# A two-layer kernel with m's norm by rows, group statistics in steps, six C products a chunk on GpSimd, and deferred transposes in layer 1

## The chip, the cores and the metric

The kernel runs on one core of a Trainium2 chip. The time is the device time of one execution in microseconds (us). PE is TensorE's matmul, PEld its weight load, DVE is VectorE, ACT ScalarE, POOL GpSimd, SP SyncE, whose queue issues most DMAs.

## The reference

`x` is 2 x 512 x 64 x 64 in float32, seen as 2 images of 4096 tokens with 512 channels. All arithmetic is float32.

```python
# layer 0: x = x + mamba(_gn(x)), _gn: group norm, 32 groups of 16 channels
xn = (xf - mu) * rsqrt(var + EPS) * ln_w + ln_b          # norm over the 512 channels of a token
xin, z = split(xn @ in_proj_w.T)                          # 1024 and 1024
xc = silu(causal_conv(xin, conv_w, 4 taps) + conv_b)
x_dbl = xc @ x_proj_w.T                                   # dt (32), B (16), C (16)
delta = softplus(dt @ dt_proj_w.T + dt_proj_b)
h = exp(delta * A) * h + delta * xc * B                   # scan over 4096 tokens, 1024 x 16 states
y = sum_n(h * C) + xc * D_skip
x = x + (y * silu(z)) @ out_proj_w.T
# layer 1: x = x + memory(_gn(x)), m: 1024 x 512
score = l2norm(xf) @ l2norm(m).T
idx = argmax(score)                                       # one row of m per token
emean = segment_sum(xf, idx) / (counts + 1e-6)
new_m = m * 0.999 + emean * 0.001
x = x + softmax(score) @ new_m
```

## The kernel before

Layer 0 goes through 32 chunks (2 images, 16 chunks of T = 256 tokens). A chunk is 32 units: 8 blocks of 128 inner channels by 4 groups of 4 states. A unit is a tile 128 x 4 x 256. For unit k:

- `decay`: ACT makes dA = exp(delta*A), four activations, into PSUM (dA, two buffers);
- `feed`: POOL multiplies bu = B * du (128 x 4 x 255) into one of LEAD = 4 buffers, four units ahead; `first` sets the first column on ACT;
- `scan`: DVE scans dA and bu, in place in PSUM, then `weigh` makes hc = dA * C on DVE;
- `gather`: PE sums hc over the states by eight transposes into yT.

Units whose number in the chunk is in `AT["aside"]` are different: the scan writes into the SBUF tile dS (tile h, pool s1, one buffer), and POOL makes the product hc one unit later. There are two buffers hc. `carry` copies of the last state are on ACT. Around the units stand the projections of the next chunk (front: pz, xi, the convolution cv, px, the softplus in `soft` with q on POOL and DVE, z), the norm of the chunk after it (`norms`), and the output product of the chunk before (`back`: po, xo, written to x1d). All of these are cut into small functions with a place: the dictionary AT gives the unit at which each is issued, a table sorted by unit and priority is worked off in the loop at L962, and the layer's engines run in exactly this order (class InOrder). That's why nearly all of layer 0 has line L36 in the profile.

Besides, at given chunks: `stats_end(1)` in chunk 0 and `end` in the chunk after an image's last one compute group statistics (`group_stats`: aggregates, two small matmuls with gmat, a reciprocal root) in one go; `unit_m` in chunks 8 to 11 normalizes a quarter of m, columns of a transposed copy mT, with a matmul by meanc for the squared lengths, and writes mnd; `clear` zeroes the two tables tab; `prelude` in the last chunk loads and normalizes the first tile of layer 1 (xf0, on POOL).

Layer 1 has two stages, in 16 tiles of TT = 512 tokens. Matching (L1108): for each of the 64 subtiles of 128 tokens 8 float32 matmuls give pc (scores, 128 x 1024); ACT copies it to sc and makes ex = exp; DVE scales ex by the reciprocal of den and takes max and max_index. One subtile later `match` makes a 128 x 128 matrix sel of equal indices (dg on ACT, pr on PE, sel on DVE) and `add_rows` gathers rows of a table, adds pe = sel x xT and counts, and scatters them back; two tables alternate. `exT_part` transposes ex of the subtile before in two halves (px, one PSUM buffer, then a copy on ACT), and a full tile exT is written to exd in DRAM. The output stage (L1173): `new_m` for 8 blocks of m from both tables (tiles e), then po = new_m x exT per tile, with exT read back from exd in two buffers (pool q3), added to xt and stored. In the first pair of tiles the blocks of new_m are interleaved with the matmuls.

Of the kernel before, what the change touches and what calls it, by code (L numbers as in the profile page):

```python
# [18 lines left out]
P = 128  # L19
# [30 lines left out]
def kernel(  # L50
# [15 lines left out]
    mT: bass.AP,  # L66
# [76 lines left out]
    def rsqrt(nc, dst, var, work):  # L143

        nc.scalar.activation(dst, var, AF.Ln, bias=epsc)
        nc.scalar.activation(dst, dst, AF.Exp, scale=-0.5)
        nc.vector.tensor_mul(work, dst, dst)
        nc.vector.scalar_tensor_tensor(work, var, EPS, work, ALU.add, ALU.mult)
        nc.vector.tensor_scalar(work, work, -0.5, 1.5, ALU.mult, ALU.add)
        nc.vector.tensor_mul(dst, dst, work)  # L150

    def group_stats(nc, st, mu, rs, pool, psum):

        mv = pool.tile([P, CB, 2], F32, tag="gs_mv", name="gs_mv")
        for cb in range(CB):
            nc.vector.bn_aggr(mv[:, cb, :], st[:, cb].rearrange("p n s -> p (n s)"))
        w = pool.tile([P, CB, 2], F32, tag="gs_w", name="gs_w")
        pm = psum.tile([P, 2, T], F32, tag="mm", name="gs_pm")
        nc.vector.tensor_copy(w[:, :, 0], mv[:, :, 0])
        nc.tensor.matmul(pm[:, 0, :CB], gmat, w[:, :, 0], start=True, stop=True)  # L160
        nc.vector.tensor_copy(mu, pm[:, 0, :CB])
        d = pool.tile([P, CB], F32, tag="gs_d", name="gs_d")
        nc.vector.tensor_sub(d, mv[:, :, 0], mu)
        nc.vector.tensor_mul(d, d, d)
        nc.vector.tensor_add(d, d, mv[:, :, 1])
        pv = psum.tile([P, 2, T], F32, tag="mm", name="gs_pv")
        nc.tensor.matmul(pv[:, 0, :CB], gmat, d, start=True, stop=True)
        d2 = pool.tile([P, CB], F32, tag="gs_d2", name="gs_d2")
        rsqrt(nc, rs, pv[:, 0, :CB], d2)
# [4 lines left out]
    with ExitStack() as l0:  # L174
# [5 lines left out]
            "u": (-10, -8, -2, 1), "xi": (-9, -4, 0, 2), "c": (-6, -3, 2, 5), "o": (-4, -2, 4, 6),  # L180
            "x": 10, "xo": 13, "z": (17, 18, 19, 21), "zo": (19, 20, 22, 26),
            "soft": (20, 21, 22, 23, 23, 25, 26, 27), "silu": 9, "early": -105,
            "aside": (2, 8, 12, 16, 26), "gate": 3,
            "norm": (-4, 3, 3, 8, 10, 11, 14, 15, 15, 16, 20, 20),
            "back": ((2, 6, 8, 11), (2, 12, 14, 18)), "end": 23, "u1": (3, 4, 7, 9),
            "xi1": (5, 6, 8, 10), "c1": (7, 9, 10, 12), "o1": (8, 10, 11, 13), "x1": 15,
            "xo1": 17, "silu1": 13, "gate1": 6, "z1": (1, 2, 3, 6),
            "soft1": ((-5, -3, -3, 1, 2, 3, 3), (3, 3, 5, 5, 5, 7, 8), (7, 7, 9, 9, 15, 17, 19)),
            "wo": (5, 1, 8, 7), "m": (2, 28, 28, 30, 31, 32), "gs": 14, "zo1": (2, 3, 4, 7),
            "norm1": (0, 0, 0, 0, 0, 1, 1, 2, 2), "affine": 0,  # L190
# [24 lines left out]
        def stats_end(b):  # L215
            group_stats(nc, st0, gmu[0][b], grs[0][b], s1, ps)
            nc.vector.tensor_mul(gsh[b], gmu[0][b], grs[0][b])
            nc.vector.tensor_scalar_mul(gsh[b], gsh[b], -1.0)
# [180 lines left out]
        stats_end(0)  # L399
# [210 lines left out]
        def back_fns(i):  # L610
# [38 lines left out]
            def end():  # L649
                if c == NCH - 1:  # L650
                    group_stats(nc, sts[b], gmu[1][b], grs[1][b], s1, ps)
                state[i].clear()
# [3 lines left out]
        def back(i):  # L656
# [10 lines left out]
            return parts + [(AT["end"], end)]  # L667

        def unit_m(q):

            s = {}
            cols = slice(q * T, (q + 1) * T)

            def load_m():
                s["m"] = s1.tile([P, CB, T], F32, tag="m", name="m")
                nc.sync.dma_start(
                    s["m"], mT[:, cols].rearrange("(cb p) k -> p cb k", p=P)
                )

            def square(h):  # L680
                sq = s1.tile([P, 2, T], F32, tag="sq", name="sqm")
                nc.scalar.activation(sq, s["m"][:, 2 * h : 2 * h + 2], AF.Square)
                if h == 0:
                    s["pn"] = ps.tile([P, 2, T], F32, tag="mm", name="pn")
                for j in range(2):
                    cb = 2 * h + j
                    nc.tensor.matmul(
                        s["pn"][:, 0], meanc, sq[:, j], start=cb == 0, stop=cb == CB - 1
                    )

            def root():
                s["r"] = s1.tile([P, 2, T], F32, tag="sq", name="rm")
                r, ss = s["r"][:, 0], s["r"][:, 1]
                nc.vector.tensor_scalar(
                    ss, s.pop("pn")[:, 0], float(C), 1e-24, ALU.mult, ALU.max
                )
                nc.scalar.activation(r, ss, AF.Ln)
                nc.scalar.activation(r, r, AF.Exp, scale=-0.5)

            def newton():  # L700
                r, ss = s["r"][:, 0], s["r"][:, 1]
                nc.gpsimd.tensor_mul(ss, ss, r)
                nc.gpsimd.tensor_mul(ss, ss, r)
                nc.gpsimd.tensor_scalar(ss, ss, -0.5, 1.5, ALU.mult, ALU.add)
                nc.gpsimd.tensor_mul(r, r, ss)

            def scale():
                m = s["m"]
                nc.gpsimd.tensor_mul(m, m, s.pop("r")[:, 0:1].to_broadcast([P, CB, T]))
                nc.sync.dma_start(mnd[:, :, cols], m)  # L710

            return list(zip(AT["m"], (
                load_m, lambda: square(0), lambda: square(1), root, newton, scale
            )))

        def clear():

            zrow = s1.tile([P, CB, T], F32, tag="m", name="zrow")
            nc.gpsimd.memset(zrow, 0.0)
            for tab in tabs:  # L720
                for kb in range(KB):
                    nc.sync.dma_start(
                        tab[kb * P : (kb + 1) * P],
                        zrow.rearrange("p n t -> p (n t)")[:, :ROW],
# [198 lines left out]
        M_AT = [len(chunks) // 4 + q for q in range(K // T)]  # L923
# [13 lines left out]
        for i in range(len(chunks)):  # L937
# [14 lines left out]
            if i > 0:  # L952
                table += [(at + n, 4, fn) for n, fn in back(i - 1)]
# [4 lines left out]
        table.append((AT["gs"], 5, lambda: stats_end(1)))  # L958
# [35 lines left out]
        end()  # L994
# [4 lines left out]
    l1 = ctx.enter_context(tc.tile_pool(name="l1", bufs=1))  # L999
    ones = l1.tile([P, P], F32, name="ones")  # L1000
    nc.gpsimd.memset(ones, 1.0)
    p3 = ctx.enter_context(tc.tile_pool(name="q3", bufs=2))
    KH = K // TT
# [13 lines left out]
    with ExitStack() as s:  # L1017
        p1 = s.enter_context(tc.tile_pool(name="p1", bufs=1))
        p2 = s.enter_context(tc.tile_pool(name="p2", bufs=2))
        ps_t = s.enter_context(tc.tile_pool(name="ps_t", bufs=1, space=PSUM))  # L1020
# [50 lines left out]
        def match(s, xT, i, fx, ix):  # L1071

            dg = p2.tile([P, P], F32, tag="dg", name="dg")
            nc.scalar.mul(dg, ident, fx)
            pr = ps_e.tile([P, TT], F32, tag="pe", name="pr")
            nc.tensor.matmul(pr[:, :P], ones, dg, start=True, stop=True)  # L1076
# [21 lines left out]
        late = None  # L1098

        def transpose_late(kh):  # L1100
            if late is not None:
# [47 lines left out]
        for kh in range(KH):  # L1149
            transpose_late(kh)  # L1150
# [100 lines left out]
```

## Time and profile before

| | us |
|---|---|
| median of three runs | 5042.65 (5036.36 to 5051.64) |
| the profiled execution | 5043.67, span 5042.0 |
| start, before the first scan | 108.9 |
| chunk 0 | 145.0 |
| a steady pair of chunks (19 and 20) | 118.5 and 116.7 |
| last chunk (31) | 131.3 |
| matching | 608.1 |
| from the last pc to the first po | 23.8 |
| output stage | 455.5 |

Busy over the span: PE 90%, DVE 80%, POOL 76%, ACT 70%. A share of the whole span is a mean over stages that have different limits, so the stages are to be read by themselves. In a line of the profile stand start, duration, engine, line, operation, output and inputs; what stands in brackets is how long the engine was idle before it and what ended that.

### The profile page before, as it was taken

How to read it: one execution, taken by the hardware profiler on the slowest of the kernel's cores; microseconds unless marked ns; L12 is line 12 of the kernel's file. 1: busy time of each engine (PE TensorE's matmuls, PEld its weight loads, DVE VectorE, ACT ScalarE, POOL GpSimd, SP SyncE). 2: the span in 40 equal slices, each digit the busy share in tenths (PEclk: the TensorE clock that was granted, in tenths of full speed). 3: DMA queues.
4: the chain of work that ended last, by engine and by line, in shares of the span. 5: the costliest groups of instructions: out<-in, count | busy, mean ns of one | idle time of the engine just before them, and what ended most of it. 6: DMA issues, size and time to landing. Idle time of an engine off the chain costs nothing. (4 is left out here: it accounts for less than half of the span.)

```text
span 5042.0 us, 64859 instructions
## 1 busy us (share of the span) xinstructions
PE 4516.4 (90%) x22704; PEld 3499.2 (69%) x22704; DVE 4053.2 (80%) x3390; ACT 3535.5 (70%) x8849; POOL 3822.8 (76%) x2821
## 2 busy tenths in 40 slices
PE   7888888898888899889888898989886899998999
PEld 6777777777777777777777777777775555553444
DVE  4899999998889999999999999999998755553100
ACT  3788888888888888788888888888886455551000
POOL 4899999999999999999999999999999322220000
PEclk9999999999999999999999999999997899998999
DMA  5131112122222112122222112211112344334453
GB/s 213 36 116 66 64 68 68 65 68 72 72 72 68 66 64 64 64 64 68 77 79 80 64 64 68 70 64 64 65 61 102 116 158 148 135 131 148 140 166 117
DMA packets 174399, 447.72 MB, mean 89 GB/s; under 512 B 23256, under 2 KB 77656, under 8 KB 169848
## 3 DMA queue, kind: packets, MB, share of 16 engines
q1 hardware_dynamic: 163832, 408.97, 23.9%
q0 software_dynamic: 10240, 34.61, 2.2%
q8 instruction: 179, 2.93, 0.2%
q14 instruction: 148, 1.21, 0.1%
HBM read 351.63 MB, written 91.88 MB: 88 GB/s over the span
## 5 line engine op out<-in xcount | busy, mean ns | idle before, releaser
L36 POOL TENSOR_TENSOR bu<-B,du 128x1020 f32<-128x1020 f32 (+1 forms) x1152 | 2466.9, 2157 | 120.4 <-DVE dA L36 101.6
L36 ACT ACTIVATE dA<-delta,A 128x256 f32<-128x256 f32 x4096 | 1957.8, 478 | 149.6 <-DVE hc L36 41.1
L36 DVE TENSOR_TENSOR_SCAN dA<-dA,bu 128x1024 f32<-128x1024 f32 x864 | 1977.9, 2289 | 38.4 <-ACT dA L36 23.2
L36 PE MATMUL yT<-ident,hc 128*128 128x128 f32 x8192 | 1062.7, 278 | 201.3 <-DVE hc L36 113.0
L36 DVE TENSOR_TENSOR hc<-dA,C 128x1024 f32<-128x1024 f32 x864 | 1058.2, 1225 | 163.7 <-PE yT L36 75.1
L36 PEld LDWEIGHTS yT<-ident,hc 128*128 128x128 f32 x8192 | 950.1, 143 | 288.4 <-DVE hc L36 139.5
L36 PE MATMUL pz<-x,win 128*128 128x256 f32 x4096 | 937.4, 382 | 33.9 <-ACT bu L36 22.4
L36 PEld LDWEIGHTS pz<-x,win 128*128 128x128 f32 x4096 | 762.8, 191 | 142.5 <-POOL bu L36 25.5
L36 PE MATMUL po<-z,wo 128*128 128x256 f32 x2048 | 521.2, 413 | 0.8 <-DVE z L36 0.8
L36 PE MATMUL cv<-xi,cd 128*128 128x256 f32 x2048 | 474.4, 385 | 28.3 <-POOL xi L36 22.2
L36 PEld LDWEIGHTS po<-z,wo 128*128 128x128 f32 x2048 | 422.7, 210 | 81.3 <-issue 15.3
L1186 PE MATMUL po<-exT,win 128*128 128x512 f32 x1024 | 444.2, 597 | 20.2 <-DVE win L1169 14.7
L36 PEld LDWEIGHTS cv<-xi,cd 128*128 128x128 f32 x2048 | 382.9, 192 | 90.5 <-POOL xi L36 27.9
L1119 PE MATMUL pc<-win,xf 128*128 128x512 f32 x960 | 432.3, 592 | 0.0
L1186 PEld LDWEIGHTS po<-exT,win 128*128 128x128 f32 x1024 | 196.0, 192 | 267.8 <-issue 267.3
L1093 POOL DMA_INDIRECT tab<-rows,ix x64 | 62.7, 979 | 418.4 <-DVE den L1134 398.7
L36 POOL TENSOR_TENSOR hc<-h,C 128x1024 f32<-128x1024 f32 x160 | 379.0, 2369 | 0.2 <-PE yT L36 0.2
L36 ACT COPY carry<-dA 128x4 f32<-128x4 f32 x810 | 129.8, 160 | 347.5 <-DVE hc L36 341.7
L36 DVE TENSOR_TENSOR_SCAN h<-dA,bu 128x1024 f32<-128x1024 f32 x160 | 364.8, 2280 | 10.4 <-ACT dA L36 8.6
L1203 DVE TENSOR_TENSOR xt<-xt,po 128x512 f32<-128x512 f32 x64 | 43.9, 686 | 388.4 <-PE po L1186 373.6
L1119 PEld LDWEIGHTS pc<-win,xf 128*128 128x128 f32 x960 | 173.0, 190 | 172.2 <-issue 172.2
L36 PE MATMUL py<-ident,ys 128*128 128x128 f32 x512 | 85.2, 291 | 188.1 <-DVE q L36 79.6
(161 smaller groups left out, 5059.5 us busy)
## 6 DMA issues: line engine op xcount, KB each, us to landing
B<-bcd SPq DMA_DIRECT2D x128, 512.0 KB, 4.0
C<-bcd SPq DMA_DIRECT2D x128, 512.0 KB, 4.0
wo<-in_out_wT_dram SPq DMA_DIRECT2D x128, 512.0 KB, 4.6
exd<-exT SPq DMA_DIRECT2D x16, 2048.0 KB, 6.4
exT<-exd SPq DMA_DIRECT2D x16, 2048.0 KB, 9.3
xl<-in_x_dram SPq DMA_DIRECT2D x32, 512.0 KB, 9.9
x<-in_x_dram SPq DMA_DIRECT2D x32, 512.0 KB, 5.2
xo<-in_x_dram SPq DMA_DIRECT2D x64, 256.0 KB, 5.7
```

What stands on the lines that cost most here:

```text
L36: ins = call(*args, **kwargs)
L1093: nc.gpsimd.indirect_dma_start(tab, at, rows, None)
L1119: nc.tensor.matmul(pc[:, cols], xf[:, cb, i * P : (i + 1) * P], mn[:, cb, cols], start=cb == 0, stop=cb == CB - 1,)
L1186: nc.tensor.matmul(pos[j, cb], mrow[:, kb, cb * P : (cb + 1) * P], ld[j][0][:, kb], start=kb == 0, stop=kb == KB - 1,)
L1203: nc.vector.tensor_add(xt[:, cb], xt[:, cb], pos.pop((j, cb)))
```

## The change

Layer 0: (1) `AT["aside"]` gets a sixth unit, 10; most other places in AT move by a unit or a few. (2) `group_stats` becomes four functions issued one unit after the other (of them the mean's copy and the aggregates stay on DVE, the rest goes to the engine given: POOL in the middle of the layer, DVE for the first and the last). (3) `unit_m` works on 8 blocks of 128 rows of m (chunks 8 to 15): lengths by an accumulating square on ACT, five small operations on POOL, the scale on ACT, four transposes, a copy, and a write to mnd. The argument mT goes. Layer 1: (4) `match` makes pr by a transpose of a broadcast copy of fx. (5) The transposes of ex follow one subtile behind as before, but in the last six iterations none is done; seven subtiles' worth then stand after the loop: two before `match`, one before `add_rows`, four after it. ex has seven buffers; exd is written from ACT's queue. For the last subtile the scaling of ex comes after max_index. (6) In the output stage, exT uses two pools in turn, four buffers.

```diff
         AT = {
-            "u": (-10, -8, -2, 1), "xi": (-9, -4, 0, 2), "c": (-6, -3, 2, 5), "o": (-4, -2, 4, 6),
+            "u": (-10, -8, -1, 1), "xi": (-9, -6, 0, 4), "c": (-5, -3, 2, 5), "o": (-2, -1, 4, 6),
...
-            "aside": (2, 8, 12, 16, 26), "gate": 3,
-            "norm": (-4, 3, 3, 8, 10, 11, 14, 15, 15, 16, 20, 20),
-            "back": ((2, 6, 8, 11), (2, 12, 14, 18)), "end": 23, "u1": (3, 4, 7, 9),
+            "aside": (2, 8, 10, 12, 16, 26), "gate": 3,
+            "norm": (-2, 2, 3, 8, 10, 10, 11, 15, 15, 17, 19, 20),
+            "back": ((0, 6, 8, 11), (3, 13, 14, 17)), "end": 18, "u1": (3, 6, 8, 9),
...
-            "wo": (5, 1, 8, 7), "m": (2, 28, 28, 30, 31, 32), "gs": 14, "zo1": (2, 3, 4, 7),
+            "wo": (6, -4, 10, 7), "m": (9, 14, 17, 20, 28, 29), "gs": 11, "zo1": (3, 4, 6, 8),
...
-    def group_stats(nc, st, mu, rs, pool, psum):
+    def group_stats(nc, engine, st, mu, rs, pool, psum):
+        s = {}
+        def means():
...
+                nc.vector.bn_aggr(mv[:, cb, :], st[:, cb].rearrange("p n s -> p (n s)"))
...
+            nc.tensor.matmul(s["pm"][:, 0, :CB], gmat, w[:, :, 0], start=True, stop=True)
+        def variances():
+            nc.vector.tensor_copy(mu, s.pop("pm")[:, 0, :CB])
...
+            engine.tensor_sub(d, mv[:, :, 0], mu)
+            engine.tensor_mul(d, d, d)
+            engine.tensor_add(d, d, mv[:, :, 1])
...
+        def roots():
+            nc.scalar.copy(s["d"], s.pop("pv")[:, 0, :CB])
+            s["v"] = s["d"]
+            nc.scalar.activation(rs, s["v"], AF.Ln, bias=epsc)
+            nc.scalar.activation(rs, rs, AF.Exp, scale=-0.5)
+        def newton():
...
+        return [means, variances, roots, newton]
...
-        def unit_m(q):
+        def unit_m(kb):
...
+                s["m"] = s1.tile([P, C], F32, tag="m", name="m")
+                nc.sync.dma_start(s["m"], m[rows])
+            def square():
...
+                nc.scalar.activation(junk[:, :C], s["m"], AF.Square, accum_out=s["ss"][:, 0:1])
             def root():
...
+                nc.gpsimd.tensor_scalar(ss, ss, 1e-24, None, ALU.max)
                 nc.scalar.activation(r, ss, AF.Ln)
                 nc.scalar.activation(r, r, AF.Exp, scale=-0.5)
...
-            def scale():
-                m = s["m"]
-                nc.gpsimd.tensor_mul(m, m, s.pop("r")[:, 0:1].to_broadcast([P, CB, T]))
-                nc.sync.dma_start(mnd[:, :, cols], m)
+            def turn():
+                nc.scalar.mul(s["m"], s["m"], s["ss"][:, 1:2])
...
+                    nc.tensor.transpose(
+                        pt[:, cb * P : (cb + 1) * P], s["m"][:, cb * P : (cb + 1) * P], ident
+                    )
+            def store():
+                mt = s.pop("m")
+                nc.scalar.copy(mt, s.pop("pt").rearrange("p a t -> p (a t)"))
+                nc.sync.dma_start(mnd[:, :, rows], mt.rearrange("p (c k) -> p c k", k=P))
...
-        M_AT = [len(chunks) // 4 + q for q in range(K // T)]
+        M_AT = [len(chunks) // 4 + kb for kb in range(KB)]
...
-        table.append((AT["gs"], 5, lambda: stats_end(1)))
+        table += [(AT["gs"] + max(n - 1, 0), -1, fn) for n, fn in enumerate(stats_end(1))]
...
+    DEFER = 6
+        p_ex = s.enter_context(tc.tile_pool(name="p_ex", bufs=DEFER + 1))
...
-            nc.scalar.mul(dg, ident, fx)
+            nc.scalar.copy(dg, fx.to_broadcast([P, P]))
             pr = ps_e.tile([P, TT], F32, tag="pe", name="pr")
-            nc.tensor.matmul(pr[:, :P], ones, dg, start=True, stop=True)
+            nc.tensor.transpose(pr[:, :P], dg, ident)
...
         def transpose_late(kh):
-            if late is not None:
-                ex, exT, i, k = late
+            if late:
+                ex, exT, i, k = late[0]
                 exT_part(ex, exT, i, kh)
-                if kh == KH - 1 and i == SUB - 1:
-                    b, t = tiles[k]
-                    nc.sync.dma_start(exd[b][t], exT)
+                if kh == KH - 1:
+                    late.pop(0)
+                    if i == SUB - 1:
+                        b, t = tiles[k]
+                        nc.scalar.dma_start(exd[b][t], exT)
...
-                    transpose_late(kh)
+                    if k * SUB + i + DEFER < len(tiles) * SUB:
+                        transpose_late(kh)
...
+                if end:
+                    scale()
...
-        add_rows(*behind, match(*behind))
+        for kh in range(2 * KH):
+            transpose_late(kh % KH)
+        sel = match(*behind)
         for kh in range(KH):
             transpose_late(kh)
+        add_rows(*behind, sel)
+        while late:
+            for kh in range(KH):
+                transpose_late(kh)
...
         for k0 in range(0, len(tiles), FIRST):
+            pool = (p3, pr3)[k0 // FIRST % 2]
...
-                exT = p3.tile([P, KB, TT], F32, tag="exT", name="exT1")
+                exT = pool.tile([P, KB, TT], F32, tag="exT", name="exT1")
```

## The prediction

> **What bounds the kernel now.** I read the page's slices first, then busy time by window (cut at the first scan of a chunk), then the timelines of DVE and POOL inside one steady chunk, and for the last 1090 us the chain of waits. Slices:
>
> ```profile
> DVE  4899999998889999999999999999998755553100
> POOL 4899999999999999999999999999999322220000
> ```
>
> For three quarters of the span DVE and POOL are both full; then neither matters. The windows say how full (PE, PEld, DVE, ACT, POOL busy, then granted PE clock):
>
> ```profile
> 2411.30:2529.80 118.50, 106.38 (x608) 91.44 (x608) 112.44 (x75) 100.22 (x260) 113.26 (x83) 0.97 0.21 68
> 2529.80:2646.50 116.70, 103.38 (x609) 89.50 (x609) 112.49 (x75) 100.50 (x260) 113.53 (x83) 1.00 0.21 69
> 1195.60:1321.50 125.90, 111.49 (x618) 95.54 (x617) 113.13 (x75) 102.19 (x264) 118.21 (x88) 0.95 0.21 72
> 2045.90:2171.50 125.60, 109.19 (x623) 94.38 (x622) 118.30 (x88) 99.89 (x254) 113.80 (x78) 0.95 0.20 64
> 3954.60:4562.70 608.10, 603.95 (x2046) 313.37 (x2047) 330.48 (x786) 303.56 (x592) 136.73 (x125) 1.00 0.42 145
> 4562.70:4586.50 23.80, 5.62 (x21) 3.05 (x19) 8.42 (x20) 4.18 (x7) 3.18 (x3) 0.68 0.48 175
> 4586.50:5042.00 455.50, 444.15 (x1024) 195.94 (x1024) 58.77 (x99) 0.00 (x0) 0.00 (x0) 0.98 0.43 141
> ```
>
> Rows 1 and 2 are a steady pair of chunks, mean 117.6 us: DVE and POOL each lack about 4 us of it, so neither has room. Row 3 is a chunk with a quarter of m's norm (8.3 over the mean), row 4 the one with the group statistics of image 0 (8.0 over). Rows 5 to 7 are layer 1: matching, PE-bound; a hole of 23.8 us with PE busy 5.6; the output product, PE-bound again.
>
> Inside a chunk (POOL and DVE, units 8 to 11):
>
> ```profile
> 2916.25 2.36 POOL L36 TENSOR_TENSOR hc<-h,C 128x1024 f32<-128x1024 f32 x1
> 2922.16 2.38 POOL L36 TENSOR_TENSOR bu<-B,du 128x1020 f32<-128x1020 f32 x1
> 2926.09 2.38 POOL L36 TENSOR_TENSOR bu<-B,du 128x1020 f32<-128x1020 f32 x1 [1.54 <-DVE dA L36]
> ...
> 2917.48 2.29 DVE L36 TENSOR_TENSOR_SCAN dA<-dA,bu 128x1024 f32<-128x1024 f32 x1
> 2920.22 1.23 DVE L36 TENSOR_TENSOR hc<-dA,C 128x1024 f32<-128x1024 f32 x1 [0.44 <-PE yT L36]
> ```
>
> POOL's own wait comes after unit 10, where it has caught up with DVE. The waits of these two chunks by releaser: POOL 4.8 us on DVE; DVE 3.3 us on PE (yT), one of them 2.4.
>
> **The change part by part.** All sums stand against the profiled execution, 5043.67 us (span 5042.0 and 1.7 around it); the median of the runs is 1.0 below it.
>
> *Sixth C product on POOL (unit 10), steady chunks.* DVE loses one hc: 1.225 us and the 0.10 gap that stands before each, 1.33. POOL gains 2.37, starting 2.33 after the instruction before. In the 116.7 us chunk POOL waits 2.0 (1.54 at unit 11, 0.35, 0.11), so its work without waits is 114.8; in the 118.5 us chunk the same sum gives 114.8. With the product it needs 117.1. DVE without its larger waits needs 115.2, afterwards 113.9. So POOL becomes the bound, 0.5 below today's mean. Against that: the products of units 8, 10 and 12 share one buffer dS (pool s1, one buffer), so scan 10 must wait for POOL's product of unit 8. That ends at 2918.61 while scan 10 starts at 2917.48 today: 1.1 us. Scan 12 waits for the product of unit 10 likewise, by my placing 0.4. DVE then needs 115.4 and, with the 1.7 us of PE wait that every second chunk has more, 117.1 there. Two engines at one limit rarely meet it: I take 117.5, bounds 117.0 and 120. Over the 23 chunks with nothing else in them: -3.5 us, bounds -14 and +55. The moved slots (AT) change no duration; they decide waits, which the trace of before can't show. I put them inside these bounds, since every wait they can remove is in the 4 us of idle, and for chunk 31 and the start at 0, within 8 either way. The same chunk has POOL's xf0 norm (8.25 us) with DVE waiting 6.75 behind it, which stays.
>
> *m by rows.* Five chunks carry m: together 617.9 us, 29.7 over the mean. Gone per quarter: on POOL 3 products of 0.725, one of 0.40 and the scale of 2.36 (5.0), on DVE 0.43 in line behind PE's pn with 0.9 of waiting, 8 PE matmul passes. Now eight chunks have a block of 128 rows: POOL 5 operations on one column, between the rows of 0.19 (128x6 copy) and 0.25 (128x32): 1.0 us; ACT square, Ln, Exp, scale, copy (0.82, 0.19, 0.21, 0.6, 0.58): 2.4 of 16 us idle; 4 transposes of PE, 0.11 each; 2 DMAs on SP, whose queue has nothing behind them that is due within their issue of 0.4 to 0.5 us. New wait: ACT's Ln stands behind POOL's max. POOL runs up to 4 us late at that slot, and behind the Ln on ACT stand the decays of the next scans; I take 0.2 per block (0 to 2). -29.7 + 8 + 2 = -20, bounds -22 and -6.
>
> *Group statistics in steps.* In row 4 DVE spends 8.5 us from 2130.83 to 2139.35, 2.3 of it waiting for PE and ACT. It keeps the four aggregates (1.92), w and mu (0.3 to 2.7); eight small operations go to POOL (1.6 us). Chunks 16 and 17 are 11.6 over the mean; I leave 3.6: -8 (0 to -11). In chunk 0 POOL waits 10.0 us at unit 14 for the same thing, DVE 3.2: -5 (0 to -8). The last statistics stay on DVE, with one ACT copy more: +0.3, left out.
>
> *Layer 1, matching.* pr becomes a transpose: one pass for two. The chain has pr x2 at 0.22 in each of 64 subtiles and PE never rests: -0.11 x 64 = -7.0. dg stays one ACT operation of 0.40 (ACT has half its time free).
>
> *Deferred transposes.* The chain at the end of matching, and one burst of px with its copy:
>
> ```profile
> 4567.17 3.61 DMA rows<-tab,ix
> 4572.47 6.95 DMA tab<-rows,ix
> 4580.69 3.01 DMA e<-tab
> 4586.50 54.31 PE po L1186 x120
> 4640.82 8.79 DMA exT<-exd
> ...
> 4541.83 0.60 PE L1066 MATMUL px<-ident,ex 128*128 128x128 f32 x4
> 4542.46 0.58 ACT L1067 COPY exT<-px 128x512 f32<-128x512 f32 x1 [1.50 <-PE px L1066]
> 4567.67 1.02 PE L1066 MATMUL px<-ident,ex 128*128 128x128 f32 x4 [3.22 <-DVE fx L1141]
> ```
>
> Six iterations lose 8 transposes (0.87 us of PE): -5.2. Seven subtiles, 14 halves, then stand between the last pc (T = 4562.65) and po. The px pool has one buffer, so PE and ACT take turns: 0.60 + 0.58 + about 0.09 of handover = 1.27 each. In the changed kernel the first load of e waits for the landing of the last exd write, which now waits for all 14. Copies start at T+2.44 (sc 1.01, ex 1.13 and 0.21 go first); the last one ends 13 periods, 0.58, one dg (0.40) and pe (0.86) later: T+20.8; landing 6.4, issue 0.9: e is issued at T+28.1, today T+17.7. So +10.4 - 5.2 = +5.2: the cover is shorter than what it should hide. [...] The rows: at 4567.67 the burst took 1.02 us after 3.2 us of PE rest, and between 2450.0 and 2458.3 PE was busy 6.23 of 8.30 us and was granted 0.50 of the clock for the next 6.8. [...] By the rows, PE busy half the time loses the clock, the period is 1.69: +10.7. I take half of the bursts slow, 1.48: +8 (5 to 11). The sooner max_index of the last subtile gains nothing under this: the scatter lands at about T+16.
>
> *Four exT buffers.* PE waits 5.52 for exT before the second pair and then runs 3.4 us at half clock (1.7 lost): -7 (0 to -7.3). The third and fourth loads now go out between loads of e; a 2 MB load takes 9.3 us, and e for k-block 2 is needed 20 us after the first: covered, thinly.
>
> Sum: -3.5 - 20 - 8 - 5 - 7 + 8 - 7 = -42.5; 5043.7 - 42.5 = 5001, by the median 5000.
>
> **Rivals.** (1) *The chunk balances on POOL worse than I think*: lag at units 8 to 13 isn't given back, chunk 118.7 instead of 117.5, in 31 chunks +37: 5037. For it: both engines full. Against: POOL's largest lags today come at 20 to 23 and are worked off. (2) *Slower: the dS buffer.* DVE waits 1.1 and 0.4 at scans 10 and 12; with POOL late by its new 2.4 the first becomes 2.5 or so, PE, with nothing to gather, loses the clock for a window more (3.4 us, 1.7 lost) and DVE's hc waits that at unit 14. 2.5 + 0.4 + 1.7 - 1.33 = +3.3 on DVE's 115.2 and the 1 us of every second chunk's wait: 119.5, +1.9 a chunk, x31 = +59: 5043.7 - 39 + 59 = 5064. It decides from 1.3 us a chunk on. For: the 1.1 us overlap is in the timeline. Against: while DVE waits there POOL has work queued, so a POOL-bound chunk loses nothing. (3) *The slots cure more*: PE's 2.4 us at unit 14 goes, the lag fits, chunk 117.0, and the end hole costs 5: 4985 to 4975.
>
> **Numbers.** Forecast 0.62, rival 1 0.15, rival 2 0.13, rival 3 0.10. About 0.3% (15 us) is what a measurement here can tell from no change. The forecast and rival 3 are faster by more, but for 0.02; rival 1 is mostly within: faster 0.73, same 0.14, slower 0.13. The range 4968 to 5052 takes in rivals 1 and 3 and leaves out most of rival 2.
>
> **What would show it.** Chunks of 117.0 to 118.0 with POOL idle under 2.5 us and DVE waiting more; chunks 8 to 15 within 2 us of the others; no 10 us POOL wait in chunk 0; matching about 12 us shorter; the hole after the last pc longer than 30 us, ended by an exd write; no wait for exT before the second pair. Steady chunks above 119 would make it wrong, as would a hole under 24.

## The result and the profile after

The changed kernel takes 5009.09 us in the median of four runs (5005.66 to 5011.13), the kernel before 5041.64 beside it (5036.36 to 5051.64): a ratio of 0.9932, with an interval of 0.9915 to 0.995. That is 32.6 us less in the medians, where 42.5 less was forecast. The profiled execution took 5005.66 us with a span of 5003.9: 38.1 less than the span of before. All the readings by stage below are of such profiled executions, and one must know how far they repeat: the same code of layer 0 took 29 us more in the profiled execution of E2 (5029.19 us) than in that of the changed kernel, 16.5 of it in chunks 8 to 15, while three further runs of E2 took 5006.91 to 5012.17. A difference of a few us between two kernels in one stage of layer 0 is therefore read by its pattern, or together with the medians.

The slices of the page of the changed kernel (tenths of each engine's busy share, 40 slices), to be laid beside the two shown of before:

```profile
DVE  5799999999999999999999999999998755553100
POOL 4899999999999999999999999999999322220000
```

Both engines are still full for three quarters of the span; the dent of DVE (three slices of 8) that was the m chunks is gone. The windows of the changed kernel (start and end, length, busy PE, PEld, DVE, ACT, POOL, granted PE clock, DMA share, GB/s): a steady pair of chunks, a chunk with m, the chunk with the group statistics of image 0, matching, the hole, the output stage.

```profile
2375.40:2493.10 117.70, 107.27 (x619) 92.67 (x618) 111.24 (x75) 99.63 (x259) 114.47 (x82) 0.99 0.21 68
2493.10:2611.10 118.00, 105.25 (x601) 90.20 (x600) 111.28 (x75) 100.55 (x261) 116.14 (x85) 0.97 0.21 68
1189.10:1307.30 118.20, 105.15 (x609) 90.58 (x609) 111.26 (x75) 102.26 (x267) 116.15 (x89) 0.99 0.22 72
2021.40:2140.50 119.10, 108.81 (x618) 93.33 (x617) 113.98 (x81) 99.28 (x256) 115.55 (x86) 0.97 0.21 70
3927.10:4520.40 593.30, 589.22 (x1941) 298.99 (x1941) 332.25 (x787) 290.11 (x582) 137.94 (x125) 1.00 0.42 145
4520.40:4555.40 35.00, 13.31 (x63) 7.78 (x62) 8.35 (x20) 10.51 (x18) 3.31 (x3) 0.70 0.51 193
4555.40:5003.90 448.50, 442.68 (x1024) 195.54 (x1024) 59.08 (x99) 0.00 (x0) 0.00 (x0) 0.99 0.42 142
```

The steady chunks are not shorter, although DVE's busy time fell from 112.4 to 111.3: rows 1 and 2 are 117.7 and 118.0, where a pair of before had a mean of 117.6. What is won stands in rows 3 and 4 (118.2 and 119.1 against 125.9 and 125.6), in matching (593.3 against 608.1) and in the output stage (448.5 against 455.5); the hole is longer, 35.0 against 23.8. By stage, in us of the two profiled executions:

| stage | before | after | difference |
|---|---|---|---|
| start | 108.9 | 105.5 | -3.4 |
| chunk 0 | 145.0 | 141.7 | -3.3 |
| 19 chunks with nothing else in them (1 to 7, 18 to 29), mean | 117.60 | 118.01 | 19 x 0.41 = +7.8 |
| chunks 8 to 15 | 969.8 | 950.9 | -18.9 |
| chunks 16 and 17 | 246.8 | 235.8 | -11.0 |
| chunks 30 and 31 | 249.6 | 250.9 | +1.3 |
| first pc to last pc | 599.9 | 585.2 | -14.7 |
| hole | 23.8 | 35.0 | +11.2 |
| output stage | 455.5 | 448.5 | -7.0 |

With the 8.2 us from the last scan to the first pc, the same in both, these differences make the 38.0 of the spans. The start was no part of the forecast; it took 105.4 to 108.0 us in the kernels below. Two rows are flattered: with the same code in these chunks, chunks 8 to 15 took 951.8 (E11), 956.4 (E8) and 967.4 us (E2), and chunks 16 and 17 took 238.9 (E11), 241.3 (E7) and 242.7 us (E2).

Where does a steady chunk wait now? The waits of DVE, and then of POOL, in the two chunks of rows 1 and 2 (engine and output, what it waited for: us in all, times, longest):

```profile
DVE hc L36 <- PE yT L36: 3.3, 5, 1.2
DVE dA L36 <- ACT dA L36: 3.2, 3, 1.4
DVE h L36 <- POOL hc L36: 2.0, 2, 1.3
...
POOL halo L36 <- ACT carry L36: 1.7, 1, 1.7
```

POOL waits 1.7 us in two chunks where it waited 4.8: it is the engine that is hardly ever free. DVE waits for three engines in turn. Its timeline around units 10 and 11 of chunk 20 (start, duration; what stands in brackets is the idle time before it and what ended that), and ACT's for the same stretch:

```profile
2529.32 2.29 DVE L36 TENSOR_TENSOR_SCAN h<-dA,bu 128x1024 f32<-128x1024 f32 x1 [0.62 <-POOL hc L36]
2534.76 2.30 DVE L36 TENSOR_TENSOR_SCAN dA<-dA,bu 128x1024 f32<-128x1024 f32 x1 [1.20 <-ACT dA L36]
```

```profile
2526.13 1.28 ACT L36 ACT_TABLE_LOAD   x1
2527.42 1.92 ACT L36 ACTIVATE z<-z 128x2048 f32<-128x2048 f32 x1
2529.26 2.00 ACT L36 ACTIVATE u<-u 128x1024 f32<-128x1024 f32 x2
2531.27 1.28 ACT L36 ACT_TABLE_LOAD   x1
2532.72 2.01 ACT L36 ACTIVATE dA<-delta,A 128x256 f32<-128x256 f32 x4
```

The first bracket is the forecast's dS wait: scan 10 may not write dS before POOL has read it for unit 8. The second was not in the forecast: ACT does its SiLU here with a table load before and after, 6.4 us in which it makes no decay, and scan 11 needs a decay made behind that. With unit 10's product gone, DVE is there sooner and waits. PE stands idle there too, for 1.94 us, since it has nothing to gather; what follows from that is seen in E3.

The end of matching, in the chain that ended last (start, us, what):

```profile
4520.53 1.01 ACT sc L1160
...
4528.50 0.67 PE px L1093 x4
4529.19 0.59 ACT exT L1094
...
4540.77 1.13 PE px L1093 x4
4541.93 0.59 ACT exT L1094
4542.54 6.26 DMA exd<-exT
...
4549.57 3.05 DMA e<-tab
...
4555.41 442.70 PE po L1231 x1024
```

The hole is ended by the write of exd (6.26 us), as forecast; before, the scatter of the table (6.95 us) ended it. And po now runs on to its end without a wait: the 5.5 us for exT before the second pair are gone.

### The profile page after: what moved, and what is told of

It reads as the page before. It is cut to its first block, busy times and chain, and to the rows that moved or that the text cites. A ratio compares the mean times of both kernels' runs of the same rounds, so it can differ in the third digit from the quotient of the medians.

```text
span 5003.9 us, 64865 instructions
## 1 busy us (share of the span) xinstructions
PE 4509.2 (90%) x22640; PEld 3483.1 (70%) x22640; DVE 4011.0 (80%) x3340; ACT 3529.2 (71%) x8885; POOL 3873.3 (77%) x2890
## 5 line engine op out<-in xcount | busy, mean ns | idle before, releaser
L36 ACT ACTIVATE dA<-delta,A 128x256 f32<-128x256 f32 x4096 | 1957.6, 478 | 151.3 <-DVE hc L36 37.8
L36 DVE TENSOR_TENSOR_SCAN dA<-dA,bu 128x1024 f32<-128x1024 f32 x832 | 1904.3, 2289 | 61.9 <-ACT dA L36 57.0
L36 PE MATMUL yT<-ident,hc 128*128 128x128 f32 x8192 | 1095.9, 283 | 215.6 <-DVE hc L36 144.3
L36 PEld LDWEIGHTS yT<-ident,hc 128*128 128x128 f32 x8192 | 965.3, 145 | 326.9 <-DVE hc L36 198.8
L36 DVE TENSOR_TENSOR hc<-dA,C 128x1024 f32<-128x1024 f32 x832 | 1019.3, 1225 | 126.0 <-PE yT L36 40.7
L36 PE MATMUL po<-z,wo 128*128 128x256 f32 x2048 | 477.2, 387 | 0.8 <-DVE z L36 0.8
L36 DVE TENSOR_TENSOR_SCAN h<-dA,bu 128x1024 f32<-128x1024 f32 x192 | 438.2, 2282 | 43.2 <-POOL hc L36 34.3
L36 POOL TENSOR_TENSOR hc<-h,C 128x1024 f32<-128x1024 f32 x192 | 454.5, 2367 | 0.0
L36 PEld LDWEIGHTS po<-z,wo 128*128 128x128 f32 x2048 | 390.3, 195 | 54.5 <-DVE z L36 1.0
```

Source lines behind the costliest of these rows:

```text
L36: ins = call(*args, **kwargs)
```

## The experiments

All edits are made to the changed kernel. "Steady" is the mean of the same 19 chunks. Where no interval is given, the kernel was run once, and its time is one execution.

**E1, the sixth product undone.** All the rest, the new places too, stays.

```diff
-            "aside": (2, 8, 10, 12, 16, 26), "gate": 3,
+            "aside": (2, 8, 12, 16, 26), "gate": 3,
```

> The changed kernel with five C products a chunk on POOL again (units 2, 8, 12, 16, 26); all else as changed. Theory A (with six, POOL is the bound at about 117.1 us of work a chunk and the sixth product brought nothing): POOL falls to 114.8 us of work, DVE rises by 1.33, steady chunks stay at 117.0 to 118.2, total 5000 to 5018. Rival B (DVE was the bound and the sixth product is a gain): chunks get 1.2 us longer, total about 5045. Rival C (the sixth product is a loss that hides other gains): chunks at 116.3 or less, total below 4985.

Measured: 4985.36 us, ratio 0.9897 (0.9881 to 0.9914). A steady chunk takes 116.99 us, chunk 0 147.5. Two consecutive chunks in the windows of E1 (columns as above):

```profile
2489.40:2606.00 116.60, 105.51 (x610) 90.98 (x609) 112.40 (x76) 99.43 (x257) 112.06 (x81) 0.99 0.21 68
2606.00:2722.80 116.80, 107.14 (x618) 92.28 (x618) 112.58 (x76) 100.61 (x260) 113.70 (x83) 0.99 0.22 68
```

DVE is busy for 1.2 us more and POOL for 2.4 less than in the changed kernel, and the chunk is a full us shorter. The chunk stands at the lower edge of theory A, but the total is some 15 us below its range. So the sixth product costs time in every steady chunk; only in chunk 0 does it gain (141.7 against 147.5).

**E9, five products at the old places.** The entries of AT for layer 0 go back to those of before, but for `m`, `gs` and `end`, which the new functions need.

```diff
-            "u": (-10, -8, -1, 1), "xi": (-9, -6, 0, 4), "c": (-5, -3, 2, 5), "o": (-2, -1, 4, 6),
+            "u": (-10, -8, -2, 1), "xi": (-9, -4, 0, 2), "c": (-6, -3, 2, 5), "o": (-4, -2, 4, 6),
...
-            "aside": (2, 8, 10, 12, 16, 26), "gate": 3,
+            "aside": (2, 8, 12, 16, 26), "gate": 3,
```

> The changed kernel with five C products and with the places of the kernel before (AT), but for those of m and of the group statistics, which stay as changed. Theory A (the moved places take away PE's lateness at unit 14 and are worth the 0.6 us a chunk between 117.6 before and 117.0 with five units and new places): steady chunks at 117.5 to 117.8, DVE waiting for yT at unit 14 in 16 or so of 19 chunks, total about 15 us above five units with new places, 5000. Rival B (something else of the change shortens the chunk): chunks 116.8 to 117.2, total about 4985.

Measured: 5014.6 us, ratio 0.9949 (0.9931 to 0.9967); steady chunks 117.64, as before the change (117.60). Against E1 that is the price of the places alone: they are worth 0.65 us a steady chunk. In the 19 steady chunks DVE's hc at unit 14 waits 28.0 us for yT with the old places and 2.2 in E1. So the changed kernel's +0.41 is the sum of -0.65 for the places and +1.02 for the sixth product (the 0.04 left is E9 against before). The sixth product at the old places was not run, so this sum is for one order of the two steps.

A second reading of E9: chunks 16 and 17 take 248.6 us, 13.3 over two steady ones, although the statistics are in steps. DVE's waits in chunk 16 of E9:

```profile
DVE hc L36 <- PE yT L36: 7.3, 4, 4.1
DVE gmu L36 <- PE gs_pm L36: 3.1, 1, 3.1
```

The mean's copy on DVE still waits for PE, in line before the scans. Steps alone gain nothing at the old places, and that is a large part of why the total is some 15 us above the expected 5000.

**E5, the sixth product at another unit.** If one aside unit too near to the others is the trouble, another place might do.

```diff
-            "aside": (2, 8, 10, 12, 16, 26), "gate": 3,
+            "aside": (2, 5, 8, 12, 16, 26), "gate": 3,
```

> The changed kernel with the sixth C product on POOL taken from unit 5 instead of unit 10. Theory A (the place costs: at unit 10 DVE's saved product only makes it wait for ACT, whose SiLU block with two table loads keeps dA of unit 11 back, and for the shared dS): DVE's waits at units 10, 11 and 14 fall from 3.1 to about 1 us a chunk, steady chunks from 118.0 to about 117.1, where POOL's work is the bound; total about 4988. Rival B (POOL's total is the bound wherever the product stands): chunks 117.8 to 118.3, total 5003 to 5012. Rival C (better than five units): chunks below 116.8, total below 4980.

Measured: 5053.74 us, ratio 1.0032 (1.0019 to 1.0046): slower than before. Steady chunks take 119.26, chunk 0 151.8. PE's timeline in one chunk of E5, and DVE's beside it:

```profile
2547.14 3.72 PE L36 MATMUL cv<-xi,cd 128*128 128x256 f32 x16 [0.55 <-POOL xi L36]
2550.70 3.62 PE L36 MATMUL po<-z,wo 128*128 128x256 f32 x16
```

```profile
2555.22 1.22 DVE L36 TENSOR_TENSOR hc<-dA,C 128x1024 f32<-128x1024 f32 x1 [2.72 <-PE yT L36]
```

PE has 32 matmuls in a row there, 7.2 us, ahead of the gather that frees an hc buffer. DVE comes 1.3 us sooner for want of unit 5's product, and only waits the longer: 49.7 us in the 19 chunks at unit 7. None of the three expectations came. It is the same thing as in the changed kernel with PE's 7.2 us in place of ACT's 6.4: the 1.3 us taken from DVE ahead of that block is handed back there, in a wait of 2.6 us a chunk.

**E4, a second dS buffer.** It takes away the wait that rival 2 stood on.

```diff
-                dA = s1.tile([P, NG, T], F32, tag="dS", name="dS")
+                dA = s2.tile([P, NG, T], F32, tag="dS", name="dS")
...
-                dAs[k] = s1.tile([P, NG, T], F32, tag="dS", name="h")
+                dAs[k] = s2.tile([P, NG, T], F32, tag="dS", name="h")
```

(s2 is a pool of two buffers; the scratch of m's square and the zero rows move into other tiles to make room.)

> The changed kernel with two buffers for dS, the tile that the scans of units 8, 10 and 12 share (the junk of m's square shares tile sq, and the zero row a dS buffer, for the room). Theory A (POOL-bound): DVE's wait of about 34 us in all for POOL's hc before these scans goes, POOL has the same work, steady chunks within 0.4 us, total 5002 to 5012. Rival B (this wait lengthens the chunk): chunks about 1.0 us shorter, total about 4978.

Measured: 5020.64 us, ratio 0.9972 (0.996 to 0.9983); steady chunks 118.07. DVE's waits in two chunks of E4:

```profile
DVE dA L36 <- ACT dA L36: 5.2, 3, 2.0
```

The wait for POOL's hc, 14.6 us over the 19 chunks in the changed kernel, is no longer among the large ones, and the wait for ACT's decay at unit 11 has grown from 20.6 to 32.5: of the 14.6 us taken from one wait, 11.9 came back at the next. The steady chunks are what theory A expected, but the total is 8.6 us above its range and 11.6 above the changed kernel's median; in the profiled execution most of the excess stands in chunks 8 to 17, 30 and 31, and its cause is open.

**E10, ACT's block made short.** Relu stands for SiLU, which takes away the table loads (1.28 us each) after chunk 0.

```diff
-                nc.scalar.activation(t, t, AF.Silu)
-            nc.scalar.preload_act_table_set("natural_log_exp_and_others")
+                nc.scalar.activation(t, t, AF.Relu)
```

> The changed kernel (six units) with Relu in place of SiLU after chunk 0 and without the two table loads, so that ACT's block at unit 9 is 2.6 us shorter; the activation is not the reference's. Theory A (six units lose because ACT's block keeps dA of unit 11 back): DVE's wait for ACT at unit 11 goes from 1.1 us a chunk to 0.3 or less, chunks from 118.0 to 117.2, where POOL's work stands, total about 4985. Rival B (POOL's work plus PE's half clock are the bound, ACT only happens to be last): chunks 117.7 to 118.2, total 4998 to 5010.

Measured: 5006.18 us, ratio 0.9935 (0.9911 to 0.9958); steady chunks 117.84. DVE's waits in two chunks of E10:

```profile
DVE hc L36 <- PE yT L36: 3.4, 4, 1.4
DVE q L36 <- POOL q L36: 2.9, 4, 0.8
DVE h L36 <- POOL hc L36: 2.6, 2, 1.5
```

The wait for ACT at unit 11 is gone, 2.6 us of ACT's work with it, and the chunk is only 0.2 us shorter, as rival B expected: DVE now waits for POOL in three places a chunk, and POOL for nothing but once 1.6. With the block gone, POOL sets the length.

**E3, POOL relieved.** The two small halo copies (0.19 us each, four pairs a chunk, 1.5 us) go to ACT.

```diff
-                nc.gpsimd.tensor_copy(xi[:, :, : TAPS - 1], src)
-                nc.gpsimd.tensor_copy(halo[:, pair], xi[:, :, T:])
+                nc.scalar.copy(xi[:, :, : TAPS - 1], src)
+                nc.scalar.copy(halo[:, pair], xi[:, :, T:])
```

> The changed kernel with the eight small copies a chunk between halo and xi (0.19 us each) on ACT instead of POOL. Theory A (POOL is the bound in the changed kernel): POOL's work falls by 1.5 us a chunk, steady chunks to about 116.5, total about 4970. Rival B (DVE waits for PE and ACT are the bound, POOL only looks full): chunks within 0.3 us, total 5000 to 5012. Rival C (ACT's in-order queue, 17 us idle but tied to DVE by the carry copies, delays the decays): chunks longer by 1 us, total about 5040.

Measured: 5009.57 us, ratio 0.9941 (0.9919 to 0.9963); steady chunks 117.91. A long and a short chunk in the windows of E3:

```profile
2494.50:2613.90 119.40, 107.70 (x610) 93.08 (x609) 111.19 (x75) 101.80 (x269) 115.74 (x77) 0.96 0.22 67
...
2852.30:2968.60 116.30, 103.93 (x610) 89.35 (x609) 111.13 (x75) 101.37 (x268) 113.22 (x75) 1.00 0.21 68
```

That is what rival B expected, and it is not for want of relief on POOL: POOL waits for DVE more than before (table below). Seven of the 19 chunks went at 116.3 us, nine at 119.0 to 119.4, with the same work. Where they part is seen around unit 13, in the timelines of PE and ACT, first in the long chunk and then in the short one:

```profile
2540.25 2.93 PE L36 MATMUL yT<-ident,hc 128*128 128x128 f32 x16 [1.96 <-DVE hc L36]
2543.11 2.07 PE L36 MATMUL pd<-xd,wdt 33*128 33x256 f32 x4
2545.22 0.47 ACT L36 ACTIVATE xd<-px,e 96x256 f32<-96x256 f32 x1 [2.77 <-PE pd L36]
...
2897.62 1.97 PE L36 MATMUL yT<-ident,hc 128*128 128x128 f32 x16 [1.97 <-DVE hc L36]
2899.52 1.13 PE L36 MATMUL pd<-xd,wdt 33*128 33x256 f32 x4
2900.68 0.47 ACT L36 ACTIVATE xd<-px,e 96x256 f32<-96x256 f32 x1 [0.86 <-PE pd L36]
```

DVE has waited 1.9 us for ACT at unit 11 in both, so PE has nothing to gather and pauses for 2 us. In the long chunk PE then runs at half clock for 6.8 us, pd takes 2.07 us instead of 1.13 and comes late, ACT waits for it and makes the next decays late, and DVE loses 1.7 us at scan 14 and 1.4 at the hc behind it. Up to scan 13 the two chunks are within 0.4 us of each other, so here the clock makes the length and not the length the clock. All 19 chunks fit: the eight with full clock there took 116.3 to 116.7 us, the two with 3.4 us of half clock 117.9, the nine with 6.8 us 119.0 to 119.4. The short chunk has the same pause and keeps its clock; why was not worked out.

In the changed kernel PE's pause there is 1.9 to 2.0 us in all 19 chunks and nine of them lose the clock; in E1 it is 1.2 to 1.3 and three do; in E10, without ACT's block, it is 0.9 to 1.6 and none does. So two limits hold the chunk of six products: POOL's own work, which E10 is left with, and PE's clock lost behind ACT's block, which E3 is left with. Both edits together were not run.

What these kernels show is best seen in one table. A wait is an idle stretch of the engine of over 0.25 us; "own" is the chunk without POOL's waits.

| kernel | steady chunk | POOL waits | POOL own | DVE waits |
|---|---|---|---|---|
| before (five, old places) | 117.60 | 2.35 | 115.25 | 2.33 |
| E9 (five, old places) | 117.64 | 2.28 | 115.36 | 2.33 |
| E1 (five, new places) | 116.99 | 1.94 | 115.05 | 1.43 |
| after (six, new places) | 118.01 | 0.96 | 117.05 | 3.93 |
| E4 (two dS) | 118.07 | 0.54 | 117.53 | 3.99 |
| E10 (no SiLU block) | 117.84 | 0.53 | 117.31 | 3.36 |
| E3 (halo on ACT) | 117.91 | 1.74 | 116.17 | 3.93 |

Six products put POOL's own time 2.0 us or more above that of five, at 117.05 to 117.5 without E3's relief, and over 116.99, the whole chunk of E1. Nothing done for DVE alone can bring the mean below that. The step is well repeated: the same steady chunk took 118.17, 117.99, 118.17 and 118.18 us in E2, E7, E8 and E11 (POOL own 117.3 to 117.5), and that of E1 took 117.02 in E6 and 116.94 in E12. The differences between after, E4, E10 and E3 are hardly larger than these repeats.

**E7, m as before.** The old unit_m, its places (2, 28, 28, 30, 31, 32), and its transposed input, in chunks 8 to 11.

```diff
-        M_AT = [len(chunks) // 4 + kb for kb in range(KB)]
+        M_AT = [len(chunks) // 4 + q for q in range(K // T)]
```

> The changed kernel with m's norm as before: four quarters in chunks 8 to 11, from the transposed copy, at the old places. Theory A (rows of m save about 20 us): chunks 8 to 15 together rise from 951 to 965 to 972. Rival B (they don't matter, the places in AT do): chunks 8 to 15 stay within 5 of 951.

Measured: 5034.71 us; chunks 8 to 15 take 971.4, in the changed kernel 950.9. Since E2 reached 967.4 with the new m, the sum alone would not decide. The pattern does: in E7 chunks 8 to 12 take 120.2, 125.2, 128.0, 122.4 and 120.7 and the next three 117.8 to 118.9, so the excess lies where m is, as it did before the change; in the changed kernel none of chunks 8 to 15 is over 120.7, and in no run with the new m is one over 122.9 (E2).

**E8, the group statistics in one go.** On DVE, at the places of before (23 and 14).

```diff
-            engine = nc.vector if b == 0 else nc.gpsimd
+            engine = nc.vector
...
-                    steps[0] = end()
+                    for fn in end():
+                        fn()
```

> The changed kernel with the group statistics in one go on VectorE at the old places (unit 14 of chunk 0, unit 23 of chunk 16); the copy of the variances by ACT stays. Theory A (steps on POOL save 8 us in chunks 16 and 17 and 5 in chunk 0): chunks 16 and 17 rise from 236 to 239 (seen in four runs) to 244 to 248, chunk 0 from 142 to about 146. Rival B (no gain): 236 to 241, and 142.

Measured: 5029.79 us; chunk 0 takes 148.0 (141.7 in the changed kernel), chunk 16 127.1 (119.1), chunk 17 116.8. In chunk 0 the loss is plain, since the changed code repeats there at 141.7 to 142.0 (E2, E7, E11). For chunks 16 and 17 the sum, 243.8, is only 1.1 above the highest repeat of the changed code (242.7 in E2); what E8 adds is chunk 16, which takes 119.0 to 122.6 us in every other run that has the steps and the new places. With E9 it says that the steps need the new places of the other work. E8 puts back two things at once, the statistics in one go and their two places, and which of them counts was not tried.

**E2, no deferral.** DEFER is 1, and the tail is that of before.

```diff
-    DEFER = 6
+    DEFER = 1
...
-        for kh in range(2 * KH):
-            transpose_late(kh % KH)
-        sel = match(*behind)
...
+        add_rows(*behind, match(*behind))
```

> The changed kernel with the transposes of ex one subtile behind to the end and the old tail (match, add_rows, then one subtile of transposes); exd writes stay on ACT's queue, ex keeps two buffers. Theory A (the hole before the output stage is 14 halves in turns of PE and ACT plus the last exd write): the hole from the last pc to the first po falls from 35.0 to about 24 us, matching grows by 6 x 0.87 = 5.2, total 5 to 6 us less, about 5003. Rival B (the scatter of the last rows sets the hole): the hole stays above 32 and the total grows by 5 or more.

Measured: 5009.74 us, ratio 0.9946 (0.9928 to 0.9963), which the medians can't tell from the changed kernel. The stages can: in the kernels that leave these alone, first to last pc repeats at 585.1 to 585.7 and the hole at 35.0 to 37.8. In E2 they are 591.3 and 23.7. Deferral saves about 6 and costs 11.3 to 14.1. The chain of E2:

```profile
4564.07 1.13 PE px L1093 x4
4565.22 0.60 ACT exT L1094
4565.84 6.74 DMA exd<-exT
...
4573.35 3.09 DMA e<-tab
```

Without deferral too, the write of exd is what the load of e waits for; so all that is added ahead of that write comes out in the hole.

**E11, pr and the exT buffers as before.** pr is again a product with ones, and exT has two buffers.

```diff
-            nc.scalar.copy(dg, fx.to_broadcast([P, P]))
+            nc.scalar.mul(dg, ident, fx)
...
-            nc.tensor.transpose(pr[:, :P], dg, ident)
+            nc.tensor.matmul(pr[:, :P], ones, dg, start=True, stop=True)
...
-            pool = (p3, pr3)[k0 // FIRST % 2]
+            pool = p3
```

> The changed kernel with pr by a matmul with ones and exT in two buffers again. Theory A: matching 7.0 us longer (592.2), output stage 7.0 longer (455.5), hole as changed (35 to 36.3). Rival B (the output stage's gain comes from the hole's longer rest or the clock, the matching's from elsewhere): either stage stays within 2 us of 585.2 and 448.4.

Measured: 5036.38 us; first to last pc 596.6 (585.2), the output stage 456.0 (448.5). The chain of E11 has the wait back:

```profile
4578.49 54.71 PE po L1234 x120
...
4633.21 8.76 DMA exT<-exd
```

Four buffers are worth 7.5 us. The pr transpose is worth 11.4 here, more than one matmul of 0.11 us in each of 64 subtiles (7.0).

**E6, a second buffer for the burst.** As E1, and after the loop every second px takes a buffer of the pool of pt, so that PE need not wait for ACT's copy.

```diff
+            if tail[0] and kh % 2:
+                px = ps_t.tile([P, C], F32, tag="pt", name="px2")
+                px = px.rearrange("p (q r) -> p q r", r=P)
+            else:
+                px = ps_x.tile([P, KBH, P], F32, tag="px", name="px")
```

> The changed kernel with five C products on POOL, and with the px tiles after the matching loop taken in turn from the px buffer and from the one of pt, which is free there. Theory A (the hole of 35 us is 14 halves in which PE and ACT take turns, then the exd write): the period falls from 1.33 (at half clock 1.79) to about 0.7, the hole to about 27, total 8 us below the run with five units alone, about 4977. Rival B (ACT's copies or the clock are the bound, or the write): the hole stays above 33, total about 4985.

Measured: 4977.71 us, ratio 0.9873 (0.9849 to 0.9897). The hole is 25.9 us against 36.1 in E1. The end of the burst in the chain of E6:

```profile
4512.70 0.59 ACT exT L1098
...
4514.03 1.08 ACT exT L1098 x2
4515.14 7.19 DMA exd<-exT
```

The last copy ends 12 us after the last pc, where it took 22 in the changed kernel: ACT now copies back to back, and px is 0.67 to the end.

**E12, the parts that pay.** E6, with unit 10 on POOL in chunk 0 alone.

```diff
-            return early(k) or k % U in AT["aside"]
+            return early(k) or k % U in AT["aside"] or k == 10
```

> Five units on POOL, but six in chunk 0, where POOL has idle time (15.8 us), and px in two banks after the loop: the version that the runs point to. Theory A (the three are independent): chunk 0 from 147.5 to about 142, total 5 to 6 us below five units with two banks, about 4972, ratio to before 0.986. Rival B (chunk 0 differs for another reason): 4978, ratio 0.9875.

Measured: 4971.75 us (4971.08 to 4973.5), ratio 0.9865 (0.9841 to 0.9888), the fastest of all: chunk 0 at 141.7, steady chunks at 116.94, the hole at 25.8.

## Why the prediction was right, and where its steps were off

The sum gave 42.5 us, the medians gave 32.6 and the spans 38.1; the direction and most of the terms hold. That the total came so near is partly luck. The sixth product was off by more than 10 us; the start, which was no part of the sum, gave back 3.4, and matching with the hole 4.5 (-3.5 where +1 was forecast).

- **Sixth product, -3.5: the term that failed.** Its two engine figures were good: POOL without waits 117.1 (measured 117.05, in repeats up to 117.5), DVE 113.9 (118.01 less 3.93 of waiting is 114.1). What was mis-sized is the step from there to 117.5, 0.4 us for two engines that don't quite meet; it was 0.96. (By its own figures, 23 chunks at 117.5 instead of 117.6 make -2.3, not -3.5.) The 19 steady chunks alone gave +7.8. And one step was wrong in kind: the places were put inside the bounds, as if they and the product could be judged together. E1 and E9 part them: -0.65 and +1.02. The sum compared the product with the idle time at the old places. The new ones had already shortened the chunk to 116.99, which is less than POOL with six products needs in the mean. What the term did not have is PE's clock lost before unit 14, which holds DVE up by 1.2 us or more in nine of the 19 chunks.
- **Rival 2 (dS).** The wait is there, 14.6 us at scan 10 in the 19 chunks, 0.8 each; the point from which it decides was put at 1.3 a chunk, and it isn't reached. E4 shows that it was no loss even so. But the chain that rival 2 drew from it, PE with nothing to gather, its clock lost and DVE held up at unit 14, did come in nine of the 19 chunks. It started one unit later, at ACT's block behind the SiLU, which was not seen: E4 takes the dS wait away and still has the wait at scan 14 in ten chunks, E10 takes ACT's block away and has it in none.
- **Rival 1** named the right place (chunk 118.7, POOL), with too large a size. Rival 3 had the places right (PE's wait at unit 14 goes, 9.7 us instead of 24.8 in the 19 chunks; E1's 116.99 is its 117.0) but not with six products.
- **m by rows, -20.** The table has -18.9, but from the lowest of four executions of that code; their mean, 956.6, makes -13.2, with the sixth product's loss in it. Before against E9, with five products and the old places in both, gives -16.5 (969.8 and 953.3). So the gain is there, inside the bounds and probably smaller than forecast; what ACT's Ln behind POOL's max costs was not parted from it.
- **Group statistics, -8 and -5.** The table has -11.0 and -3.3; the mean of four executions, 239.7 for chunks 16 and 17, makes the first -7.1. The reason given was incomplete: it was the steps that were to gain it, but E9 has the steps and gains nothing in either place (248.6, and 145.1 in chunk 0). Chunk 0 needs the sixth product besides (147.5 without, in E1). POOL's 10 us wait is gone; what then sets chunk 0 was not worked out.
- **pr, -7.0.** Measured between -8.6 (before against E2) and -11.4 (E11): more than the matmul of 0.11 us that was saved in each of 64 subtiles (pr has 128 in the kernel before and 64 in the changed one). PE's order differs among these kernels, and what the rest is stays open.
- **Deferral, +8** as -5.2 and +13.2. Measured by E2 -6.1 and +11.3, which is +5.2, with the other holes up to +8.0. The burst's mean period, taken as 1.48, was 1.49: of 13, eight at 1.33, one at 1.57 and four at 1.79. The last copy ended 22.1 us after the last pc, where the sum at that period has 23.5, since pe and the last dg fell beside the copies and not behind them.
- **exT buffers, -7.** Measured -7.0; undone, 7.5.

Of what was to show it, POOL's wait in chunk 0, the matching, the hole ended by an exd write and the missing exT wait came as told, and so did the m chunks but for chunk 11 (120.7, 2.7 over the others); the chunks of 117.0 to 118.0 were just missed.

How much of the burst would be slow: the forecast set a period of 1.27 us, by the durations at full clock, beside one of 1.69, by rows of the kernel before in which PE had half its clock; that half of the bursts would be slow was the author's estimate. Three stretches of the burst in the changed kernel (columns as above), the second up to the fall of the clock:

```profile
4527.27:4530.69 3.42, 1.86 (x13) 1.15 (x12) 0.76 (x2) 1.34 (x3) 0.79 (x1) 1.00 0.25 94
4530.69:4534.10 3.41, 1.59 (x11) 1.11 (x11) 0.00 (x0) 1.59 (x3) 0.19 (x1) 1.00 1.03 428
4534.10:4537.51 3.41, 2.06 (x10) 1.26 (x9) 0.00 (x0) 1.17 (x2) 0.00 (x0) 0.50 0.57 233
```

In the 3.41 us before the fall PE is busy for 1.59 us, with pauses of 0.68 us from one px to the next and none longer; then the granted clock is 0.50, px goes from 0.67 to 1.13 us and the period from 1.33 to 1.79. So the burst lost its clock with PE busy about half the time, as the forecast had taken it from its rows, but after eight periods at 1.33. Why the clock fell at that moment no run shows.

## What to carry to other kernels

Where two engines both have next to no idle time, work out the receiver's own time without its waits before moving an operation to it, and compare that with the chunk as the other edits will leave it, not as it is (here POOL's 117.05 us with E1's 116.99, not with 117.60). Time taken from DVE ahead of a fixed block of another engine (ACT's table loads and SiLU, 6.4 us; 32 matmuls of PE, 7.2 us) came back here as a wait at that block, and in nine of 19 chunks the pause of 1.9 to 2.0 us was followed by half clock on PE besides, so try the moved work and the moved places each alone. When taking one limit away gains nothing (E10 and E3, 117.84 and 117.91 after 118.01), look for a second one of the same height before calling the first harmless. The work put off behind the loop cost its chain here and not its busy time, since a write that everything waits for stands at its end (5.2 us of PE put off, 11.3 more of hole); a second buffer for the burst gave most of it back (36.1 to 25.9).

## What the runs showed of the hardware

- In the changed kernel's burst PE was granted 0.50 of its clock after 3.41 us in which it was busy for 1.59, with no pause over 0.68 us in them (above). In the steady chunks 4.1 (E10) to 5.9 us (E5) of each went at half clock, 4.5 in the kernel before and 5.4 in the changed one. The amount alone does not order the kernels: E1, the shortest of the table, has 5.2.
- In E3 the same work took 116.3 us where PE kept its clock around unit 13, and 119.0 to 119.4 where it ran 6.8 us at half clock there; the clock fell first.
- POOL's bu products of 128 x 1020 had a mean of 2.383 us in the changed kernel and 2.404 in E2, with the same code; 32 of them make 0.7 us a chunk. The runs do not say why.
- One code took 950.9 and 967.4 us for chunks 8 to 15 in two executions (the changed kernel's and E2's).
